# A selective-scan kernel: states and channels are laid out 4 x 32 on the partitions, and TensorE makes the scan's input

## The chip, the cores and the metric

The kernel runs on one core of one Trainium2 chip. A core has five engines, each with its own instruction queue worked off in order: PE (TensorE, matrix products; its weight loads are listed apart as PEld), DVE (VectorE), ACT (ScalarE), POOL (GpSimd) and SP (SyncE, which here only issues transfers). They meet by semaphores alone. Data lie in SBUF (128 partitions) and, for what PE writes, in PSUM (128 partitions, 8 banks of 512 fp32 columns). The metric is the device time of one execution in microseconds; of several runs the median counts.

## The reference, cut to what matters

The input is `x` of 64 channels x 256 time steps x 128 frequencies. A first layer runs two stages of bidirectional Mamba blocks, one along time and one along frequency; a second layer, a convolutional LSTM, follows and isn't touched here. For each direction of each stage:

```
u  = x * rsqrt(mean(x^2)) * norm_w
x, z = split(u @ in_proj)                      # 128 channels each
x  = silu(depthwise_conv4(x))
dt, B, C = split(x @ x_proj)                   # 4, 16, 16
dt = softplus(dt @ dt_proj + bias)             # 128 channels
for t:  h = exp(dt_t * A) * h + dt_t * B_t * x_t     # 128 channels x 16 states
        y_t = sum over the 16 states of h * C_t
y  = (y + x * Dp) * silu(z)
out = y @ out_proj
```

For each token the recurrence has 128 channels x 16 states = 2,048 values. All is fp32.

## The kernel before

**Tiling.** A stage (`Stage`) has 32,768 tokens in 64 chunks of 512 tokens (2 sequences of 256 in the time stage, 4 of 128 in the frequency stage). A chunk has two directions `d`, and each direction 8 slots of 128 partitions x 1,024 columns, so 16 slots `S` a chunk, 1,024 a stage, 2,048 in all. On the partitions lie 16 states x 8 channels; a slot's two column halves `j` are two groups of channels, 512 tokens each. A direction's eight slots are numbered by `k` (0 to 3) and `r` (0, 1).

**What a slot needs.** `inputs` (L546): PE spreads `dt*x` (tile `dtx`, 128 channels x 512 tokens) over the 16 states with the constant 0/1 matrix `sel`, two products of 64 rows x 512 columns, into the PSUM tile `bx` (two banks, three buffers). `times_b` (L580) multiplies `bx` by `B`, which was spread over the partitions by a transfer; 24 of 32 slots do this on DVE. The other 8 are "swapped" (L556): ACT copies `bx` into the SBUF tile `dA`, POOL multiplies there, and the decays go into `bx` instead. `decays` (L561): ACT computes exp(dt*A) from `rep`, the step sizes replicated over the states by a transfer (`spread_dt`, L456; 512 KB, one per slot, 7 buffers), into one of four `dA` tiles; the first column of every sequence is set to zero so that sequences don't mix. `recur` (L590): one DVE scan over 1,024 columns makes `h` (5 buffers). `outputs` (L608): POOL multiplies `h` by `C`. `add_up` (L613), every second slot: PE sums the states with the matrix `fold` into the PSUM tile `y`, four products of 512 columns, each on its own 32-column tile of the array. After eight slots DVE's `gate` (L634) multiplies `y` by `zs`, and `close_a`, `close_b`, `keep` (L641 to L675) make the stage's output.

**What a chunk needs before.** `HEAD` (L70) is a table of (slot, step): the steps that prepare the next chunk, placed among the slots of the current one (16 is the next chunk's first slot). `load`, `squares`, `means`, `rms`, `normalise` make the normalised input; `project_x`, `project_z` the projections; `silus` loads ACT's silu table and applies it to both directions' `xs` and `zs`. Softplus is made from abs, relu, exp and ln on ACT and three identity products on PE that add the parts up (`softplus_a`, `softplus_b`, `softplus_sum`, L392 to L424). `dt_away` writes `dt` to DRAM, from where `spread_dt` fetches it; `times_x` (POOL) makes `dtx`; `project_bc` makes B and C and writes them to DRAM, from where `spread_bc` fetches them replicated. All transfers are issued by SP, in the program's order.

**Order.** `run` (L686) writes the order out by hand; nothing reorders it. At slot S it issues: times_b(S+1), recur(S), at S mod 8 = 2 the gate, outputs(S-1), inputs(S+2), decays(S+2), the table's steps of slot S, skip, add_up, close_a or close_b with keep, then the steps of slot S+0.5. Each engine works off its share in this order, so an instruction that waits holds all that stand behind it on its engine. In the slot of `silus` the decays of two slots go ahead, in the next slot none.

Other PSUM tiles come from `mm` (one bank; one buffer). `first` (L471) prepares the first chunk of each stage.

Of the kernel before, what the change touches and what calls it, by code (L numbers as in the profile page):

```python
# [42 lines left out]
DL = P // NS  # L43
NK = 4
NG = 4 * NK
# [13 lines left out]
NREP = 7  # L59
RESPOND = 6  # L60
NH = 5
LAG = 2
SWAPPED = (2, 5, 9, 14, 18, 21, 25, 30)
EXP_AND_LN = "natural_log_exp_and_others"
SILU = "silu_and_others"
EDGES = (0, 1, LF - 2, LF - 1)
# [5 lines left out]
    (-8.5, "squares"),  # L72
    (-4.5, "means"),
    (-4.5, "rms"),
    (-3, "normalise"),
    (0, "project_x", 0),
    (1.5, "project_z", 0),
    (4, "project_z", 1),
    (5, "project_x", 1),
    (5, "silus"),  # L80
    (7.5, "project_bc", 0),
    (8, "softplus_a", 0),
    (8.5, "softplus_b", 0),
    (8.5, "spread_bc", 0, 0),
    (10.5, "softplus_sum", 0),
    (10.5, "dt_away", 0),
    (11.5, "times_x", 0),
    (12, "spread_bc", 0, 1),
    (12, "spread_dt", 0, 0),
    (12, "spread_dt", 0, 1),  # L90
    (12.5, "project_bc", 1),
    (12.5, "spread_dt", 0, 2),
    (13, "softplus_a", 1),
    (13, "softplus_b", 1),
    (13.5, "spread_dt", 0, 3),
    (14.5, "spread_dt", 0, 4),
    (15, "softplus_sum", 1),
    (15.5, "dt_away", 1),
    (16, "spread_dt", 0, 5),
    (16.5, "spread_dt", 0, 6),  # L100
    (16.5, "spread_dt", 0, 7),
    (17, "spread_dt", 1, 0),
    (17.5, "spread_bc", 1, 0),
    (19, "spread_dt", 1, 1),
    (20.5, "times_x", 1),
    (21, "spread_dt", 1, 2),
    (22, "spread_dt", 1, 3),
    (23, "spread_bc", 1, 1),
    (23, "spread_dt", 1, 4),
    (24, "spread_dt", 1, 5),  # L110
    (26.5, "spread_dt", 1, 6),
    (26.5, "spread_dt", 1, 7),
)

SECOND = tuple(
    (max(slot, 16), *step) for slot, *step in HEAD if step[0] == "spread_dt" and step[1:] > [0, 3]
) + (
    (14, "softplus_a", 1),  # L120
    (15, "softplus_b", 1),
    (15, "softplus_sum", 1),
    (15, "dt_away", 1),
    (16, "spread_bc", 1, 0),
    (16, "spread_bc", 1, 1),
    (17, "times_x", 1),
)


class Mamba:  # L130
# [3 lines left out]
    def __init__(self, ctx, tc, cols, room, d):  # L134
# [4 lines left out]
        self.mask = cp.tile([P, 2, NK, DL], F32, name="mask")  # L139
        self.sel = cp.tile([P, 2, NK, P], F32, name="sel")  # L140
        self.fold = cp.tile([P, NK, 32], F32, name="fold")
# [4 lines left out]
        self.A = cols[:, 12 : 12 + 4 * NG].rearrange("p (i g) -> p i g", i=4)  # L146
# [78 lines left out]
    def spreads(self):  # L225

        nc, mask = self.nc, self.mask
        nc.vector.tensor_add(mask.rearrange("p r k d -> p (r k d)"), self.ident[:, 0:C], self.ident[:, C:P])
        for r in range(2):
            for k in range(NK):  # L230
                nc.vector.tensor_copy(
                    self.sel[:, r, k].rearrange("p (s d) -> p s d", s=NS),
                    mask[:, r, k].unsqueeze(1).to_broadcast([P, NS, DL]),
                )

    def folds(self, ps):

        nc = self.nc
        pf = ps[:, 0 : 32 * NK].rearrange("p (k n) -> p k n", k=NK)
        for k in range(NK):  # L240
            nc.tensor.matmul(
                pf[:, k], lhsT=self.sel[0:32, 0, k], rhs=self.ident[0:32, 0:32], start=True, stop=True
            )
        nc.vector.tensor_copy(self.fold, pf)
# [13 lines left out]
class Stage:  # L258
# [8 lines left out]
    def __init__(self, ctx, m, stage, L, X, src, moments, gates):  # L267
# [12 lines left out]
        self.ps_mm = ctx.enter_context(tc.tile_pool(name=n + "mm", bufs=1, space=PSUM))  # L280
        self.ps_bx = ctx.enter_context(tc.tile_pool(name=n + "bx", bufs=3, space=PSUM))
        self.ps_y = ctx.enter_context(tc.tile_pool(name=n + "y", bufs=1, space=PSUM))

# [3 lines left out]
        self.zeros = fixed.tile([P, 2, self.nseq, 1], F32, name="zeros", tag="zeros")  # L287
        nc.gpsimd.memset(self.zeros, 0.0)
        self.dA = []
        for k in range(NRING):  # L290
            self.dA.append(fixed.tile([P, 2, self.nseq, L], F32, name=f"dA{k}", tag=f"dA{k}"))
# [76 lines left out]
    def project_x(self, ch, d):  # L368
        i = 2 * self.stage + d
        px = self.mm("px")  # L370
        xs = self.wk.tile([P, NTOK], F32, name="xs", tag="xs", bufs=3)
        self.shifted(px, i)
        self.nc.scalar.activation(xs, px, AF.Identity, bias=self.m.cb[:, i : i + 1])
        self.at["xs", ch, d] = xs

    def project_z(self, ch, d):
        pz = self.mm("pz")
        self.gated(pz, 2 * self.stage + d)
        zs = self.wk.tile([P, NTOK], F32, name="zs", tag="zs", bufs=4)
        self.nc.scalar.copy(zs, pz)  # L380
        self.at["zs", ch, d] = zs

    def silus(self, ch):
        nc = self.nc
        nc.scalar.preload_act_table_set(SILU)
        for n in ("xs", "zs"):
            for d in range(2):
                t = self.at[n, ch, d]
                nc.scalar.activation(t, t, AF.Silu)
        nc.scalar.preload_act_table_set(EXP_AND_LN)  # L390

    def softplus_a(self, ch, d):  # L392


        nc, m, wk = self.nc, self.m, self.wk
        i = 2 * self.stage + d
        pv = self.mm("pv")
        nc.tensor.matmul(pv, lhsT=m.Wdt[i], rhs=self.at["xs", ch, d], start=True, stop=True)  # L398
        e = wk.tile([P, NTOK], F32, name="e", tag="e")
        nc.scalar.activation(e, pv, AF.Abs, bias=m.dtb[:, i : i + 1])  # L400
        nc.scalar.activation(pv, pv, AF.Relu, bias=m.dtb[:, i : i + 1])
        nc.scalar.activation(e, e, AF.Exp, scale=-1.0)  # L402
        self.at["e", d], self.at["pv", d] = e, pv

    def softplus_b(self, ch, d):
        nc, wk = self.nc, self.wk
        w = wk.tile([P, NTOK], F32, name="w", tag="w")
        lw = wk.tile([P, NTOK], F32, name="lw", tag="lw")
        nc.scalar.activation(w, self.at["e", d], AF.Identity, bias=1.0)
        nc.scalar.activation(lw, w, AF.Ln)  # L410
        nc.scalar.activation(w, w, AF.Identity, scale=-1.0, bias=1.0)  # L411
        self.at["w", d], self.at["lw", d] = w, lw

    def softplus_sum(self, ch, d):

        nc, pv = self.nc, self.at["pv", d]
        parts = [self.at[n, d] for n in ("e", "w", "lw")]
        for n, t in enumerate(parts):
            nc.tensor.matmul(  # L419
                pv, lhsT=self.m.ident, rhs=t, start=False, stop=n == len(parts) - 1, skip_group_check=True  # L420
            )
        dt = self.wk.tile([P, NTOK], F32, name="dt", tag="dt", bufs=2)
        nc.scalar.copy(dt, pv)  # L423
        self.at["dt", d] = dt  # L424

    def dt_away(self, ch, d):

        there = self.dram.tile([32, 2, 2, NTOK], F32, name="there", tag="there")
        for r in range(4):
            self.nc.sync.dma_start(out=there[:, r % 2, r // 2], in_=self.at["dt", d][32 * r : 32 * r + 32])  # L430
        self.at["there", ch, d] = there

    def times_x(self, ch, d):
        dtx = self.wk.tile([P, NTOK], F32, name="dtx", tag="dtx", bufs=3)
        self.nc.gpsimd.tensor_mul(dtx, self.at["dt", d], self.at["xs", ch, d])  # L435
        self.at["dtx", ch, d] = dtx

    def project_bc(self, ch, d):
# [4 lines left out]
        self.nc.scalar.copy(t, pb)  # L443
        away = self.dram.tile([NBC, NTOK], F32, name="away", tag="away")
        self.nc.sync.dma_start(out=away, in_=t)
        self.at["away", ch, d] = away

    def spread_bc(self, ch, d, h):
        t = self.wk.tile([P, NTOK], F32, name="BC"[h], tag="BC"[h], bufs=3)
        away = self.at["away", ch, d]  # L450
        self.nc.sync.dma_start(
            out=t, in_=away[NS * h : NS * (h + 1)].unsqueeze(1).to_broadcast([NS, DL, NTOK])
        )
        self.at["BC"[h], ch, d] = t

    def spread_dt(self, ch, d, n):  # L456
        k, r = divmod(n, 2)
# [3 lines left out]
            out=t, in_=there[DL * k : DL * (k + 1), r].unsqueeze(0).to_broadcast([NS, DL, 2, NTOK])  # L461
        )
        self.at["rep", ch, d, n] = t
# [7 lines left out]
    def first(self):  # L471
# [4 lines left out]
        banks = [self.ps_bx.tile([P, 2, NTOK], F32, name="bx", tag="bx") for _ in range(3)]  # L476
# [10 lines left out]
        if time:  # L487
            m.dt(0, self.mm("pw"))
            m.load(False)
        x, z = {}, {}  # L490
        for d in range(2):
            x[d] = self.wk.tile([P, NTOK], F32, name="xs", tag="xs", bufs=3)
            z[d] = self.wk.tile([P, NTOK], F32, name="zs", tag="zs", bufs=4)
            self.at["xs", 0, d], self.at["zs", 0, d] = x[d], z[d]
        self.shifted(banks[0][:, 0], s)
        nc.scalar.activation(x[0], banks[0][:, 0], AF.Silu, bias=m.cb[:, s : s + 1])
        nc.scalar.preload_act_table_set(EXP_AND_LN)
        self.softplus_a(0, 0)
        if time:
            m.decay()  # L500
            m.spreads()
# [3 lines left out]
        self.softplus_b(0, 0)  # L505
        self.spare = [banks[0][:, 1]]
# [756 lines left out]
```

## Time and profile before

| | us |
|---|---|
| median of 3 runs | 7327.76 (7315.61 to 7332.9) |
| span of the profiled execution | 7324.0 |
| first scan's start to the last's | 48.7 to 6629.7 |
| ConvLSTM, after the second stage | from about 6640 to the end |
| PE busy | 6510.4 (89%) |
| DVE busy | 6924.8 (95%) |
| ACT busy | 6119.2 (84%) |
| POOL busy | 6703.3 (92%) |

The profile gives one execution. Its groups of instructions show the line, engine, operation, the tile written and those read, the shapes and the count; after the bar the busy time and the mean duration in ns; after the next bar the engine's idle time just before these instructions and what ended it. The timeline lists instructions in order of time: start, length (of several in a row together), engine, line, operation, tiles and count, and in brackets the idle time before it and what released it. An fp32 product shows as two MATMUL and two LDWEIGHTS instructions, here called its two halves. Matmuls overlap in the array, and a duration includes the filling of the pipe, so start-to-start distances tell what they cost. "64*128 64x512" is a product on a tile of 64 rows by 128 columns of the array, with 512 columns streamed.

### The profile page before, as it was taken

The numbers are of one execution on the slowest core, as the hardware profiler recorded it, in microseconds if no ns is written. First come the engines' busy times: TensorE is split into PE (matmuls) and PEld (weight loads), VectorE is DVE, ScalarE is ACT, GpSimd is POOL, SyncE is SP. The second block draws the span as 40 slices with busy tenths as digits, with TensorE's granted clock in tenths as the row PEclk, the third lists the DMA queues.
The fourth block names the chain that finished last, engine by engine and source line by source line (L and its number), as shares of the span: only waits on it lengthen the run. The fifth ranks groups of instructions, "written<-read, shape, count | busy, mean of one in ns | idle before, by whom it ended". The sixth has DMA issues, their size and how long they took to land. (4 is left out here: it accounts for less than half of the span.)

```text
span 7324.0 us, 86482 instructions
## 1 busy us (share of the span) xinstructions
PE 6510.4 (89%) x25104; PEld 2254.8 (31%) x25104; DVE 6924.8 (95%) x4684; ACT 6119.2 (84%) x11092; POOL 6703.3 (92%) x3410
## 2 busy tenths in 40 slices
PE   8888888888888888887898898888888888888999
PEld 2222222222222222222222222222222222226887
DVE  7999999999999999997999999999999999996887
ACT  7888889888898888987999999988998989983333
POOL 6999999999999999997999999999999999995554
PEclk9999999999999999999999999999999999999999
DMA  7888888888888888886888888878888788882000
GB/s 171 206 206 208 199 210 204 205 207 205 210 203 209 206 204 207 204 210 159 208 211 209 210 215 200 208 197 202 206 201 204 199 209 198 205 202 62 15 15 17
DMA packets 505887, 1359.47 MB, mean 186 GB/s; under 512 B 72772, under 2 KB 129732, under 8 KB 505416
## 3 DMA queue, kind: packets, MB, share of 16 engines
q1 hardware_dynamic: 505416, 1353.93, 74.6%
q8 instruction: 205, 3.36, 0.2%
q14 instruction: 266, 2.18, 0.1%
HBM read 1228.34 MB, written 92.27 MB: 180 GB/s over the span
## 5 line engine op out<-in xcount | busy, mean ns | idle before, releaser
L611 POOL TENSOR_TENSOR h<-h,C 128x1024 f32<-128x1024 f32 x2048 | 4797.5, 2366 | 32.4 <-DVE h L598 22.0
L598 DVE TENSOR_TENSOR_SCAN h<-dA,bx 128x1024 f32<-128x1024 f32 x1536 | 3443.8, 2269 | 0.0
L553 PE MATMUL bx<-dtx,sel 64*128 64x512 f32 x8192 | 2578.7, 653 | 364.8 <-DVE h L598 362.5
L588 DVE TENSOR_TENSOR bx<-bx,B 128x1024 f32<-128x1024 f32 x1536 | 1863.7, 1213 | 178.8 <-PE bx L553 178.2
L576 ACT ACTIVATE dA<-rep,cols 128x510 f32<-128x510 f32 (+1 forms) x3072 | 2021.7, 710 | 11.3 <-DMA rep<-there 11.3
L585 POOL TENSOR_TENSOR dA<-dA,B 128x1024 f32<-128x1024 f32 x512 | 1205.9, 2355 | 161.9 <-ACT dA L570 155.8
L553 PEld LDWEIGHTS bx<-dtx,sel 64*128 64x128 f32 x8192 | 733.3, 190 | 1888.1 <-issue 1070.5
L620 PE MATMUL y<-h,fold 128*32 128x512 f32 x8192 | 1239.5, 618 | 12.6 <-POOL h L611 10.9
L598 DVE TENSOR_TENSOR_SCAN h<-bx,dA 128x1024 f32<-128x1024 f32 x512 | 1167.9, 2281 | 15.4 <-POOL dA L585 15.4
L570 ACT COPY dA<-bx 128x1024 f32<-128x1024 f32 x512 | 518.5, 1013 | 352.7 <-PE bx L553 338.0
L576 ACT ACTIVATE bx<-rep,cols 128x510 f32<-128x510 f32 (+1 forms) x1024 | 705.5, 689 | 33.7 <-ACT bx L573 0.4
L398 PE MATMUL pv<-xs,wdt 128*128 128x512 f32 x512 | 341.2, 753 | 261.5 <-ACT bc L443 167.5
L620 PEld LDWEIGHTS y<-h,fold 128*32 128x32 f32 x8192 | 188.5, 109 | 933.5 <-issue 504.0
L435 POOL TENSOR_TENSOR dtx<-dt,xs 128x512 f32<-128x512 f32 x256 | 327.6, 1280 | 54.2 <-ACT dt L423 33.7
L364 PE MATMUL pz<-unp,wz 64*128 64x512 f32 x504 | 283.5, 642 | 91.0 <-ACT X L669 54.0
L360 PE MATMUL px<-unp,g 128*128 128x512 f32 x504 | 283.8, 644 | 9.5 <-DMA unp<-xn 7.0
L419 PE MATMUL pv<-e,ident 128*128 128x512 f32 x512 | 288.1, 645 | 3.4 <-ACT e L402 3.4
L441 PE MATMUL pb<-xs,wbc 128*32 128x512 f32 x504 | 260.9, 599 | 15.6 <-ACT made L809 15.6
L419 PE MATMUL pv<-w,ident 128*128 128x512 f32 x512 | 262.6, 594 | 6.1 <-ACT w L411 6.1
L419 PE MATMUL pv<-lw,ident 128*128 128x512 f32 x512 | 262.3, 594 | 0.0
L361 PE MATMUL px<-unp,g 128*128 128x512 f32 x504 | 257.8, 592 | 0.0
L1150 POOL TENSOR_TENSOR y<-v,X 128x512 f32<-128x512 f32 x32 | 40.6, 1270 | 230.7 <-DVE v L1148 230.7
(206 smaller groups left out, 7066.0 us busy)
## 6 DMA issues: line engine op xcount, KB each, us to landing
rep<-there SPq DMA_DIRECT2D x2048, 512.0 KB, 7.8
B<-away SPq DMA_DIRECT2D x256, 256.0 KB, 8.9
there<-dt SPq DMA_DIRECT2D x1024, 64.0 KB, 3.3
C<-away SPq DMA_DIRECT2D x256, 256.0 KB, 3.4
unp<-xn SPq DMA_DIRECT2D x504, 64.0 KB, 3.3
away<-bc SPq DMA_DIRECT2D x256, 64.0 KB, 4.1
u<-in_x SPq DMA_DIRECT2D x128, 64.0 KB, 8.9
out<-y SPq DMA_DIRECT2D x32, 256.0 KB, 2.0
```

The source lines that it names most:

```text
L360: nc.tensor.matmul(self.seqs(px), lhsT=m.G1[i], rhs=self.unp[:, :, first : first + L], start=True, stop=False)
L398: nc.tensor.matmul(pv, lhsT=m.Wdt[i], rhs=self.at["xs", ch, d], start=True, stop=True)
L419: nc.tensor.matmul(pv, lhsT=self.m.ident, rhs=t, start=False, stop=n == len(parts) - 1, skip_group_check=True)
L435: self.nc.gpsimd.tensor_mul(dtx, self.at["dt", d], self.at["xs", ch, d])
L553: self.nc.tensor.matmul(bx[:, j], lhsT=self.m.sel[rows, r, k], rhs=dtx[rows], start=True, stop=True)
L570: nc.scalar.copy(dA.rearrange("p j n l -> p j (n l)"), bx)
L576: nc.scalar.activation(dA[:, j, :, live], self.seqs(rep[:, j])[:, :, live], AF.Exp, scale=m.A[:, i, g : g + 1])
L585: self.nc.gpsimd.tensor_mul(bx, bx, b)
L588: self.nc.vector.tensor_mul(bx, bx, b)
L598: self.nc.vector.tensor_tensor_scan(h.rearrange("p j n -> p (j n)")[:, step], dA[:, step], bx[:, step], 0.0, ALU.mult, ALU.add,)
L611: self.nc.gpsimd.tensor_mul(h, h, self.at["C", ch, d].unsqueeze(1).to_broadcast([P, 2, NTOK]))
L620: nc.tensor.matmul(y[32 * r : 32 * r + 32], lhsT=m.fold[:, k], rhs=hs[r % 2][:, r // 2], start=False, stop=k == NK - 1, skip_group_check=True,
```

## The change

The layout becomes 4 states x 32 channels on the partitions. A direction's eight slots are numbered `q` (0, 1) and `b` (0 to 3): `b` is a block of 32 channels, and a slot holds states 4j + 2q + g for j = 0 to 3 (partitions) and g = 0, 1 (columns). Its 1,024 columns are i (half of the tokens, one PSUM bank each), g, and 256 tokens as 4 groups `u` of 64.

- `times_b` and `swapped` go. PE makes dt*x*B in one go: `turn` transposes `dtx` (tokens onto the partitions, `dtxT`, copied to SBUF by ACT) and B (tile `bt` in PSUM); `diagonal` (DVE, four calls per direction, each 128 x 1,024) multiplies B's turned columns with a mask of two stacked 64 x 64 identities, which gives 64 x 64 diagonal blocks `D`. `inputs` then multiplies `dtxT` (64 tokens x 32 channels, the weights) with the diagonal blocks (64 x 128, streamed): 32 products of 128 columns per slot on tiles of 64 rows by 32 columns, of which the array has eight.
- `bx` has two buffers instead of three, `mm` two instead of one, `bt` one: the eight banks are full.
- `spread_dt`: a replicated tile holds two channel blocks and serves four slots; two transfers per direction instead of eight (3 buffers). `spread_c` fetches C as 128 x 1,024, two per direction; B is not fetched. `dtx` and `bc` are written in the order (u, i, c); `away` is written by four transfers instead of one.
- `add_up` comes every fourth slot and adds four slots: 8 products of 512 columns on four column tiles, two on each. It is issued ahead of the table's steps. `h` has 7 buffers instead of 5.
- Softplus is ACT's own function with a table load of its own: one activation per direction; the identity products go. Both directions' `pv` products follow `silus` directly (`step_sizes`).
- `HEAD` is written anew; `silus` stands at slot 4 instead of 5.

```diff
-NREP = 7
+NREP = 3
-NH = 5
+NH = 7
...
 HEAD = (
...
+    (-2, "project_x", 0),
+    (-1, "project_z", 0),
+    (-1, "project_z", 1),
+    (0, "project_x", 1),
+    (4, "silus"),
+    (4, "step_sizes"),
+    (5, "softplus"),
+    (6, "project_bc", 0),
+    (6, "dt_away", 0),
+    (6.5, "dt_away", 1),
+    (7, "times_x", 0),
+    (8.5, "spread_dt", 0, 0),
+    (9, "spread_c", 0, 0),
+    (10, "turn", 0),
+    (11, "diagonal", 0, 0, 0),
+    (12, "spread_dt", 0, 1),
+    (12, "project_bc", 1),
+    (12.5, "times_x", 1),
+    (13, "diagonal", 0, 0, 1),
+    (13.5, "spread_c", 0, 1),
+    (15, "diagonal", 0, 1, 0),
+    (17, "diagonal", 0, 1, 1),
+    (17.5, "spread_dt", 1, 0),
+    (17.5, "spread_c", 1, 0),
+    (18, "turn", 1),
+    (19, "diagonal", 1, 0, 0),
+    (20, "spread_dt", 1, 1),
+    (21, "diagonal", 1, 0, 1),
+    (21.5, "spread_c", 1, 1),
+    (23, "diagonal", 1, 1, 0),
+    (25, "diagonal", 1, 1, 1),
...
-        self.ps_mm = ctx.enter_context(tc.tile_pool(name=n + "mm", bufs=1, space=PSUM))
-        self.ps_bx = ctx.enter_context(tc.tile_pool(name=n + "bx", bufs=3, space=PSUM))
+        self.ps_mm = ctx.enter_context(tc.tile_pool(name=n + "mm", bufs=2, space=PSUM))
+        self.ps_bx = ctx.enter_context(tc.tile_pool(name=n + "bx", bufs=2, space=PSUM))
...
+    def soft(self, ch, d):
...
+        self.nc.scalar.activation(dt, self.at["pv", d], AF.Softplus, bias=self.m.dtb[:, i : i + 1])
...
+    def turn(self, ch, d):
...
+        for u in range(NU):
+            own = slice(P * u, P * (u + 1))
+            nc.tensor.transpose(pt[:, own], dtx[:, own], m.ident)
+        for u in range(NU):
+            nc.tensor.transpose(bt[:, u], bc[0:NS, P * u : P * (u + 1)], m.ident[0:NS, 0:NS])
+        t = self.wk.tile([P, NU, P], F32, name="dtxT", tag="dtxT", bufs=2)
+        nc.scalar.copy(t.rearrange("p u d -> p (u d)"), pt)
...
+    def diagonal(self, ch, d, q, h):
...
+        self.nc.vector.tensor_mul(
+            D,
+            self.m.mask.unsqueeze(1).unsqueeze(1).to_broadcast([P, n, 2, W]),
+            b.unsqueeze(3).to_broadcast([P, n, 2, W]),
+        )
...
     def inputs(self, S):
...
-        for j in range(2):
-            rows = slice(C * j, C * j + C)
-            self.nc.tensor.matmul(bx[:, j], lhsT=self.m.sel[rows, r, k], rhs=dtx[rows], start=True, stop=True)
+        bx = self.ps_bx.tile([P, 2, 2, NU, W], F32, name="bx", tag="bx")
+        for u in range(NU):
+            for j in range(NJ):
+                for i in range(2):
+                    rows = slice(W * i, W * (i + 1))
+                    self.nc.tensor.matmul(
+                        bx[DB * j : DB * (j + 1), i, :, u],
+                        lhsT=dtxT[rows, u, DB * b : DB * (b + 1)],
+                        rhs=D[rows, u, j],
+                        start=True,
+                        stop=True,
+                    )
...
     def add_up(self, S):
...
+        for g in range(2):
+            for b in range(NB):
+                nc.tensor.matmul(
+                    y[DB * b : DB * (b + 1)].rearrange("p (i t) -> p i t", i=2),
+                    lhsT=self.m.fold,
+                    rhs=hs[b][:, g],
...
-            if 0 <= S + 1 < last:
-                self.times_b(S + 1)
...
+            if S % 4 == 1 and 4 < S <= last + LAG:
+                self.add_up(S - LAG)
```

## The prediction

> **What bounds the kernel now.** I read the page's first two parts, then the groups of instructions, then the waits of DVE, then the timeline of a few slots.
>
> ```profile
> span 7324.0 us, 86482 instructions
> ...
> PE 6510.4 (89%) x25104; PEld 2254.8 (31%) x25104; DVE 6924.8 (95%) x4684; ACT 6119.2 (84%) x11092; POOL 6703.3 (92%) x3410
> ...
> L611 POOL TENSOR_TENSOR h<-h,C 128x1024 f32<-128x1024 f32 x2048 | 4797.5, 2366 | 32.4 <-DVE h L598 22.0
> L598 DVE TENSOR_TENSOR_SCAN h<-dA,bx 128x1024 f32<-128x1024 f32 x1536 | 3443.8, 2269 | 0.0
> ...
> L588 DVE TENSOR_TENSOR bx<-bx,B 128x1024 f32<-128x1024 f32 x1536 | 1863.7, 1213 | 178.8 <-PE bx L553 178.2
> ...
> L585 POOL TENSOR_TENSOR dA<-dA,B 128x1024 f32<-128x1024 f32 x512 | 1205.9, 2355 | 161.9 <-ACT dA L570 155.8
> ```
>
> DVE and POOL are both nearly full; the multiplication by B, which the change takes away, sits on both (1,536 times on DVE, 512 on POOL). DVE's only large wait is for PE's `bx`, 178 us. The scans tell the length of a chunk (16 slots):
>
> ```profile
> L598 DVE TENSOR_TENSOR_SCAN h<-dA,bx x1536: 2256/2273/2285, 48.7 to 6629.7; 128x1024 f32<-128x1024 f32 x192
> ```
>
> From 48.7 to 6629.7 us is 6,581 us, or 51.4 us for each of 128 chunks. The timeline gives what one instruction really costs, from its start to the next one's:
>
> ```profile
> 3001.61 0.67 DVE L636 TENSOR_TENSOR yz<-y,zs 128x512 f32<-128x512 f32 x1
> ...
> 3002.19 1.22 DVE L588 TENSOR_TENSOR bx<-bx,B 128x1024 f32<-128x1024 f32 x1
> ...
> 3003.19 1.13 PE L553 MATMUL bx<-dtx,sel 64*128 64x512 f32 x4
> ...
> 3003.32 2.28 DVE L598 TENSOR_TENSOR_SCAN h<-dA,bx 128x1024 f32<-128x1024 f32 x1
> ...
> 3004.25 1.06 PE L620 MATMUL y<-h,fold 128*32 128x512 f32 x8
> ...
> 3005.24 0.70 PE L327 MATMUL pm<-sq,ones 128*128 128x256 f32 x2
> ...
> 3005.51 1.21 DVE L588 TENSOR_TENSOR bx<-bx,B 128x1024 f32<-128x1024 f32 x1
> ...
> 3006.63 4.45 DVE L598 TENSOR_TENSOR_SCAN h<-dA,bx 128x1024 f32<-128x1024 f32 x2
> ...
> 3006.93 1.04 PE L441 MATMUL pb<-xs,wbc 128*32 128x512 f32 x2
> ```
>
> A scan takes 2.19 (3003.32 to 3005.51), a B multiplication 1.12 (to 3006.63), a gate 0.58. A chunk has 16 scans, 12 B multiplications on DVE and 2 gates: 35.0 + 13.4 + 1.2 = 49.6 us. So 1.8 us of 51.4 is idle, about 0.3 of that the pause between the stages. POOL has 16 x 2.37 + 4 x 2.36 + 2 x 1.28 + 0.73 = 50.7 us: the two are balanced. How DVE comes to wait is seen here:
>
> ```profile
> 2077.19 2.07 PE L398 MATMUL pv<-xs,wdt 128*128 128x512 f32 x2 [1.82 <-ACT bc L443]
> ...
> 2079.19 1.73 PE L553 MATMUL bx<-dtx,sel 64*128 64x512 f32 x4
> ...
> 2080.97 1.23 DVE L588 TENSOR_TENSOR bx<-bx,B 128x1024 f32<-128x1024 f32 x1 [1.23 <-PE bx L553]
> ```
>
> PE runs in order: a `pv` product that waits for ACT holds the `bx` behind it, and DVE loses 1.23 us, even with three `bx` buffers.
>
> **The change, what DVE and POOL gain.** The 12 multiplications go; 8 `diagonal` calls come, each a 128x1024 tensor_tensor with one operand in PSUM like L588, so 1.12 each (from 1.08, twice the 0.54 by which it exceeds a gate of half the columns, to 1.22, L588's whole duration). DVE's chunk: 35.0 + 9.0 + 1.2 = 45.2 us, 4.4 less. POOL's falls to 37.9 + 2.6 + 0.7 = 41.2: no bound. If idle time stayed as it is, the kernel would save 128 x 4.4 = 563 us.
>
> **What ACT and the queues gain.** The swapped slots' four copies (1.04) go, and six of seven softplus instructions (about 0.6 each, twice), against one table load more (1.28) and two copies of `dtxT` (0.58). ACT was 84% busy: off the path by itself, but see below. Replicated step sizes fall from 16 transfers of 512 KB a chunk to 4; B's 2 go; C's 2 of 256 KB become 4 of 512 KB; `away` is written in 8 issues, not 2; SP issues some 30 where it issued some 36. ACT waited 11.3 us in all for `rep`, so this is worth that at most.
>
> **What PE pays.** A call of `inputs` was two products of 512 columns (four instructions: an fp32 product is two, each with a weight load). It becomes 32 products of 128 columns on 64x32 tiles, so 64 instructions and 64 loads. Two halves of one product take 0.86 of streaming (successive L419 products start at 3001.38 and 3002.24), 0.43 a half; L1027 at 240 columns is 160.5/768 = 0.21. Both scale to 0.107 for 128 columns. Each of eight tiles has 8 halves: 0.86 us if the eight run side by side, 6.9 us if none do. No row shows eight. The nearest: the fold's eight halves on four column tiles take 1.06 where the same shape on one tile (L441, two halves) takes 1.04; `bx`'s four on two row tiles take 1.13, as two of L360 do. Both directions overlap whole, so I take 0.87, and keep 1.72 (four at a time) and 6.9 as ends. An `inputs` call holds PE 1.06 now (3003.19 to 3004.25); it would hold it 1.06 - 0.86 + 0.87, about 1.1.
>
> The Trainium skill, "TensorE: Matmul & The Clock Gate", Part 3 (packing small matmuls), speaks against it: matmuls start and end in strict program order, only weight loads are pulled ahead. By that rule a product's second half would hold the tiles behind it, 32 x 0.11 = 3.5 us a call, an estimate that makes the kernel about 11.4 ms. The fold's row disagrees: in order it would need over 1.7 us, not 1.06. Part 1 (the clock gate) of the same page states a floor of about 25 ns between matmul starts: 64 x 0.025 = 1.6 us, an estimate that adds 5 x 0.73 us to the chain below and gives some 7,930 us.
>
> **The new wait.** `bx` has two buffers where it had three, so `inputs(S+2)` starts only when scan S ends; and there is work on PE and ACT that must follow in order. Per chunk the longest such row goes from the end of scan 0 to the start of scan 7. On PE: inputs 1.1, project_x 1.92 (2066.09 to 2068.01 in the timeline), inputs 1.1, add_up (two products on each of four tiles: 0.99 + 0.86 = 1.85), inputs 1.1, turn (eight halves of 128 columns 0.86 + 0.2, and four narrow ones; 1.4, between 0.6 and 1.9), close_a (0.86 + 2 x 0.43 + 0.2 = 1.92), inputs 1.1, close_b 1.0: 12.5 us. Then ACT: keep 0.95 (L661, two), the decays of slots 6 and 7 (four, 2.55), table load 1.29, first silu 0.62: 5.4. Then PE: two `pv` products 1.9, inputs(7) 1.1, add_up(3) 1.85, for scan 7 writes the `h` buffer (seven of them) that add_up(3) reads: 4.85. Four hand-overs of 0.12 (1.13 - 1.06 and 0.05 until the other engine starts) are 0.5, and the project_z ahead on PE costs some 0.5. Sum 23.8 us. DVE's own work in that stretch is 6 scans, 3 diagonals and a gate: 13.1 + 3.4 + 0.6 = 17.1. It waits 6.7 us. Elsewhere PE has slack: its chunk is 16 x 1.07 + 23.7 (fold 7.4, px 3.8, pz 2.1, pv 1.9, pb 2.1, means 0.6, turn 2.8, po 2.9, rounded) = 40.8 of DVE's 45.2.
>
> **The sum.** 45.2 + 6.7 + 0.3 (pause) + 0.3 (small waits, a third of today's) = 52.5 us a chunk, against 51.4: 128 x 1.1 = 141 us more. The span of 7,324.0 becomes 7,465; the median shown is 7,327.8, 3.8 above that span, so 7,469, which I give as 7,470. Prologue and the ConvLSTM (from 6,640 us on) keep their time within some 10 us.
>
> **Rivals.**
> Faster: the chain is shorter than I add up. It decides at 17.1 + 5.6 = 22.7 us, for then 45.2 + 5.6 + 0.6 is 51.4. With turn at 0.6 and neither hand-overs nor late start it is 22.0: 128 x 0.7 saves 90, 7,240. If add_up(3) is done in time, too, it is 20.2 and the stall 3.1: 48.9 us, 7,010; without any stall 6,610. For it: the chain is only 1.1 us above the point. Against it: 0.87 for `inputs` is already the floor.
> Eight tiles run four at a time: 1.72 + 0.2 a call; PE's chunk is 16 x 1.92 + 23.7 = 54.4, and it still waits some 4 us for ACT and DVE: 58.7, so 7,328 + 128 x 7.3 = 8,260. For it: nothing here shows loads and matmuls at 128 in 3 us (the ConvLSTM has 5,330 in 564 us, 9 a us). Against it: the fold's rows.
> No overlap between halves of different products: 3.5 a call, 23.7 + 16 x 3.7 = 83 us, 11.4 ms. Against it, again the 1.06.
> Hidden anyway: PE's extra work falls into DVE's scans and the chain just balances, within 0.2% (what a measurement of this kernel can tell from no change, 15 us, is 0.1 us a chunk).
>
> **How the numbers follow.** Forecast 0.52 (its own range 7,350 to 7,750: the chain from 22.9 to 26), faster 0.26, four at a time 0.14, no overlap 0.05, balance 0.03. Slower is 0.52 + 0.14 + 0.05 = 0.71. From 7,130 to 8,250 leaves out a third of the faster case and most of the two slow tile cases, 0.19 to 0.2.
>
> **What the profile will show.** The `inputs` line has 131,072 matmuls; if I am right about the tiles, 64 of them lie within about 1.1 us. The diagonals take 1.2 each, 1,024 of them. DVE's wait is put down to PE at the scan, once a chunk, at slot 7, for some 5 to 7 us; PE's wait to ACT's silu of `xs` at `pv`. POOL and the DMA share fall (DMA to half). I am wrong if `inputs` calls take 2 us or more, if PE's instructions come in late (gaps inside a call), or if slot 7 comes without a gap.

## The result, and the profile after

The changed kernel takes 7879.8 us (median; 7858.0 to 7885.2), the kernel before it 7324.9 in the same series: the ratio is 1.0748 (95% interval 1.0729 to 1.0767). The forecast was 7,470, slower by 141 us; it is slower by 555. The first lines of the page:

```profile
span 7880.5 us, 324564 instructions
...
PE 6410.5 (81%) x148488; PEld 3602.5 (46%) x148488; DVE 6363.7 (81%) x4166; ACT 4921.4 (62%) x8918; POOL 5571.1 (71%) x2898
...
PEclk8889999988899898988999898999889899998999
...
L583 DVE TENSOR_TENSOR_SCAN h<-dA,bx 128x1024 f32<-128x1024 f32 x2048 | 4614.8, 2275 | 1018.8 <-PE y L598 812.6
L555 PE MATMUL bx<-D,dtxT 64*32 64x128 f32 x131072 | 2578.3, 292 | 880.1 <-DVE h L583 872.5
...
L444 DVE TENSOR_TENSOR D<-mask,bt 128x1024 f32<-128x1024 f32 x1026 | 1226.0, 1195 | 9.7 <-PE bt L431 9.7
...
L363 PE MATMUL pv<-xs,wdt 128*128 128x512 f32 x512 | 452.2, 1035 | 510.3 <-ACT xs L357 508.8
```

DVE does less (6,364 us instead of 6,925) and stands still more; no engine is full. The waits of DVE (engine, line, what it waited for; us in all, times, longest) say for whom:

```profile
DVE h L583 <- PE y L598: 812.6, 166, 7.9
DVE yz L614 <- PE y L598: 291.2, 249, 4.4
DVE h L583 <- ACT dA L575: 198.4, 68, 13.0
```

Most of it is for `y`, the fold of `add_up`; the second line, the gate's wait, was not in the forecast at all. Where the waits lie in a chunk is read best from the distances between the starts of successive scans. This table is worked out from the trace: the mean, over the 56 middle chunks of each of the two stages, of the distance from scan n to scan n+1 of a chunk (column n). Columns that show DVE's own work to within 0.2 us are left out (e7 alone has more there, 4.0 us a chunk in all); the first row is that own work (scan 2.20, diagonal 1.11, gate 0.58), 45.2 us a chunk.

| kernel | us | chunk | 0 | 2 | 6 | 7 | 8 | 10 | 14 |
|---|---|---|---|---|---|---|---|---|---|
| DVE's own work | | 45.2 | 2.20 | 2.78 | 2.20 | 3.31 | 2.20 | 2.78 | 2.20 |
| changed kernel | 7880 | 55.5 | 2.36 | 3.82 | 9.11 | 3.32 | 2.20 | 4.17 | 3.05 |
| e1, PE kept at work | 7631 | 53.4 | 2.29 | 3.84 | 7.23 | 3.32 | 2.20 | 3.93 | 3.12 |
| e2, `pv` later | 7571 | 53.0 | 2.59 | 3.85 | 2.27 | 7.14 | 2.20 | 4.42 | 3.09 |
| e3, `add_up` ahead | 7758 | 54.6 | 2.24 | 3.05 | 9.88 | 3.32 | 2.20 | 2.78 | 3.66 |
| e5, eight `h` buffers | 7805 | 55.1 | 5.20 | 4.08 | 7.33 | 3.32 | 2.56 | 2.89 | 2.21 |
| e6, ACT ahead | 7796 | 54.8 | 2.25 | 4.08 | 7.57 | 3.32 | 2.20 | 4.39 | 3.55 |
| e7, `inputs` twice | 9785 | 70.4 | 3.81 | 6.46 | 10.29 | 3.32 | 2.37 | 6.74 | 5.93 |
| e8, four moves | 7571 | 53.1 | 6.08 | 4.67 | 2.29 | 3.30 | 3.60 | 2.78 | 2.67 |
| e9, transfers in four parts | 7842 | 55.3 | 2.34 | 3.82 | 9.06 | 3.32 | 2.20 | 4.17 | 2.91 |
| e10, e8 and e9 together | 6896 | 47.8 | 2.20 | 3.33 | 2.28 | 3.30 | 3.62 | 2.78 | 2.69 |
| e11, e5 and e9 together | 7484 | 52.5 | 2.80 | 3.92 | 7.42 | 3.32 | 2.54 | 2.81 | 2.20 |
| e12, e2, e3 and e9 together | 7324 | 51.2 | 2.25 | 3.17 | 2.20 | 7.56 | 2.20 | 3.25 | 3.04 |
| e13, e10 with `pb` later | 6901 | 47.8 | 2.20 | 3.32 | 2.28 | 3.30 | 3.58 | 2.78 | 2.75 |

The changed kernel's excess of 10.3 us a chunk lies in column 6 (6.9: ahead of scan 7), 2 (1.0: first gate), 10 (1.4: second gate), 14 (0.85: scan 15) and 0 (0.2). Two stretches of its timeline show how (start, length, engine, line, operation, tiles and count; in brackets the idle time before it and what released it). First the wait ahead of scan 7:

```profile
2288.88 1.15 PE L555 MATMUL bx<-D,dtxT 64*32 64x128 f32 x64 [0.48 <-DVE h L583]
...
2293.98 3.78 PE L363 MATMUL pv<-xs,wdt 128*128 128x512 f32 x4 [3.96 <-ACT xs L357]
...
2297.69 1.96 PE L555 MATMUL bx<-D,dtxT 64*32 64x128 f32 x64
...
2299.58 1.92 PE L598 MATMUL y<-h,fold 128*32 128x512 f32 x16
...
2301.62 2.29 DVE L583 TENSOR_TENSOR_SCAN h<-dA,bx 128x1024 f32<-128x1024 f32 x1 [7.40 <-ACT dA L575]
```

PE stands still for 4 us until ACT's silu, then `pv`, `inputs(7)` and `add_up(3)` follow in order, and scan 7 starts 0.12 us after the last. (The wait is named after ACT because the decays of slot 8 end at the same moment; those of slot 7 were done at 2292.0.) `inputs` took 1.15 us at 2288.88 and 1.96 after the standstill, `pv` 3.78 where the forecast had 1.9. The windows of that stretch tell why (each line has a stretch and its length; for PE, PEld, DVE, ACT and POOL the busy time, and in brackets the instructions; then the granted clock, the DMA share and GB/s):

```profile
2294.00:2296.00 2.00, 2.00 (x3) 0.96 (x4) 0.22 (x1) 1.98 (x4) 1.70 (x1) 0.50 0.26 102
2296.00:2298.00 2.00, 2.00 (x19) 0.49 (x25) 0.00 (x0) 1.63 (x3) 1.08 (x2) 0.50 0.25 102
...
2300.00:2302.00 2.00, 2.00 (x56) 0.82 (x56) 0.38 (x1) 1.58 (x4) 0.00 (x0) 1.00 0.08 33
```

Second, the gate at slot 10:

```profile
2251.63 1.20 DVE L444 TENSOR_TENSOR D<-mask,bt 128x1024 f32<-128x1024 f32 x1
2251.77 1.96 PE L555 MATMUL bx<-D,dtxT 64*32 64x128 f32 x64 [1.02 <-DVE h L583]
2252.75 2.28 DVE L583 TENSOR_TENSOR_SCAN h<-dA,bx 128x1024 f32<-128x1024 f32 x1
2253.66 2.63 PE L598 MATMUL y<-h,fold 128*32 128x512 f32 x16
...
2256.40 0.69 DVE L614 TENSOR_TENSOR yz<-y,zs 128x512 f32<-128x512 f32 x1 [1.38 <-PE y L598]
```

`inputs(11)` may start only when scan 9 ends, since `bx` has two buffers; `add_up(7)` stands behind it. DVE has a diagonal and scan 10 to do meanwhile, 3.3 us. At full clock the two calls take 3.1 us and would just be covered; here they take 4.5, for the clock is at half again:

```profile
2248.33:2251.74 3.41, 1.16 (x64) 0.89 (x64) 3.41 (x3) 3.36 (x7) 2.48 (x2) 1.00 0.50 120
2251.74:2255.15 3.41, 3.38 (x72) 1.90 (x76) 3.29 (x2) 0.00 (x0) 2.62 (x3) 0.50 0.26 55
```

All 112 middle chunks agree. In 5 of them the clock was full from the end of scan 9 to the end of the fold, and the gate didn't wait at all; in the 107 others it waited 1.04 to 2.38 us, 1.34 on average. Scan 15, which waits for `add_up(11)` to free its `h` buffer, was 0.01 us late on average in the 61 chunks in which the clock was full from the end of scan 12 on, and 1.69 us in the 51 others.

### The profile page after: what moved, and what is told of

Read it like the earlier page. It is cut to its first block, busy times and chain, and to the rows that moved or that the text cites. A ratio compares the mean times of both kernels' runs of the same rounds, so it can differ in the third digit from the quotient of the medians.

```text
span 7880.5 us, 324564 instructions
## 1 busy us (share of the span) xinstructions
PE 6410.5 (81%) x148488; PEld 3602.5 (46%) x148488; DVE 6363.7 (81%) x4166; ACT 4921.4 (62%) x8918; POOL 5571.1 (71%) x2898
## 3 DMA queue, kind: packets, MB, share of 16 engines
q1 hardware_dynamic: 300616, 674.33, 25.3%
## 4 chain that ended last, share of the span: by engine, by line
PE 33%; DVE 9%; ACT 5%; issue 4%; DMA 1%; POOL 1%; SPq 0%; DVEq 0%; POOLq 0%; ACTq 0%
PE bx L555 9%; DVE h L583 7%; PE cv L1003 6%; PE y L598 5%; PE pv L363 3%; ACT dA L575 2%; DVE D L444 2%; PE px L328 2%; PE pz L332 2%; PE px L329 1%; ACT L353 1%; ACT X L647 1%; PE po L629 1%; PE po L623 1%; POOL h L589 1%
## 5 line engine op out<-in xcount | busy, mean ns | idle before, releaser
L583 DVE TENSOR_TENSOR_SCAN h<-dA,bx 128x1024 f32<-128x1024 f32 x2048 | 4614.8, 2275 | 1018.8 <-PE y L598 812.6
L555 PE MATMUL bx<-D,dtxT 64*32 64x128 f32 x131072 | 2578.3, 292 | 880.1 <-DVE h L583 872.5
L555 PEld LDWEIGHTS bx<-D,dtxT 64*32 64x32 f32 x131072 | 1994.9, 112 | 2351.7 <-DVE h L583 1007.3
L575 ACT ACTIVATE dA<-rep,cols 128x510 f32<-128x510 f32 (+1 forms) x4096 | 2657.0, 709 | 12.0 <-DVE h L583 6.0
L444 DVE TENSOR_TENSOR D<-mask,bt 128x1024 f32<-128x1024 f32 x1026 | 1226.0, 1195 | 9.7 <-PE bt L431 9.7
L598 PE MATMUL y<-h,fold 128*32 128x512 f32 x8192 | 1085.1, 648 | 6.0 <-POOL h L589 6.0
L363 PE MATMUL pv<-xs,wdt 128*128 128x512 f32 x512 | 452.2, 1035 | 510.3 <-ACT xs L357 508.8
L341 ACT ACTIVATE xs<-px,cols 128x512 f32<-128x512 f32 x252 | 173.6, 689 | 573.7 <-PE px L329 573.7
L614 DVE TENSOR_TENSOR yz<-y,zs 128x512 f32<-128x512 f32 x256 | 176.9, 691 | 291.2 <-PE y L598 291.2
L572 ACT COPY dA<-zeros 128x4 f32<-128x4 f32 (+1 forms) x1024 | 194.9, 190 | 3.3 <-DVE h L583 3.2
L373 ACT ACTIVATE dt<-pv,cols 128x512 f32<-128x512 f32 x256 | 172.5, 687 | 25.3 <-issue 20.5
```

The source lines that it names most:

```text
L363: self.nc.tensor.matmul(pv, lhsT=self.m.Wdt[i], rhs=self.at["xs", ch, d], start=True, stop=True)
L444: self.nc.vector.tensor_mul(D, self.m.mask.unsqueeze(1).unsqueeze(1).to_broadcast([P, n, 2, W]), b.unsqueeze(3).to_broadcast([P, n, 2, W]),)
L555: self.nc.tensor.matmul(bx[DB * j : DB * (j + 1), i, :, u], lhsT=dtxT[rows, u, DB * b : DB * (b + 1)], rhs=D[rows, u, j], start=True, stop ...
L575: nc.scalar.activation(dA[:, :, g, :, live], rep[:, :, :, live], AF.Exp, scale=m.A[:, k, n : n + 1])
L583: self.nc.vector.tensor_tensor_scan(h[:, step], dA[:, step], bx[:, step], 0.0, ALU.mult, ALU.add)
L598: nc.tensor.matmul(y[DB * b : DB * (b + 1)].rearrange("p (i t) -> p i t", i=2), lhsT=self.m.fold, rhs=hs[b][:, g], start=False, stop=q == ...
```

## The experiments

Theories: the chain theory of the forecast (DVE waits where a row of ordered work on PE, and on ACT ahead of it, is longer than its own); as rivals, that PE has too much to do wherever it stands, so that waits only move, and that the clock alone is to blame. Column numbers are those of the table; what the expectations call the wait at slot 7 is column 6, and the one of scan 15 is column 14.

**e1: PE kept at work while it waits for ACT**

```diff
-    def step_size(self, ch, d):
+    def step_size(self, ch, d, extra=0):
...
         self.at["pv", d] = pv = self.mm("pv")
+        for _ in range(extra):
+            self.nc.tensor.matmul(
+                pv, lhsT=self.m.ident, rhs=self.unp.rearrange("p n l -> p (n l)")[:, 0:NTOK], start=True, stop=True
+            )
...
-            self.step_size(ch, d)
+            self.step_size(ch, d, 0 if d else 4)
```

> Four more 128x128 products of 512 columns stand ahead of the first pv product and write into the same PSUM tile, which pv then overwrites; they need nothing of ACT, so PE has 3.4 us of work in the 4.0 us in which it stood still there. Clock theory (the standstill is followed by a stretch at half the granted clock, in which two pv products took 3.78 instead of 1.9 us and inputs 1.96 instead of 1.16): pv 1.9, inputs 1.16, slot 7 comes 2.6 us sooner, 128 x 2.6 = 330 us less, about 7,550. Rival (the clock falls for another reason, such as the load over a longer time, or pv is slow in itself): nothing gained, 7,880 to 7,930, the longer end if the extra products hold up pv by 0.4 us.

7631.2 us, ratio 1.0421 (1.0401 to 1.0440): 249 us sooner, with 1,008 more matmul instructions. The same place in its windows, and its group of `pv` products:

```profile
1663.70:1665.70 2.00, 1.93 (x6) 0.69 (x6) 0.31 (x1) 1.98 (x5) 1.61 (x1) 1.00 0.25 102
1665.70:1667.70 2.00, 2.00 (x77) 1.20 (x80) 0.00 (x0) 1.99 (x3) 1.09 (x2) 1.00 0.26 106
```

```profile
L367 PE MATMUL pv<-xs,wdt 128*128 128x512 f32 x512 | 255.2, 620 | 59.0 <-ACT xs L357 57.5 <-ACT xs L500 1.6
```

The clock is full, a `pv` instruction has a mean of 620 ns instead of 1,035, and column 6 falls by 1.9. So the half clock at `pv` comes of the standstill; 1.9 of the 2.6 us expected came. Column 10 fell by only 0.24: in 103 of the 112 chunks the clock was still at half there.

**e2: `pv` behind `inputs(7)`**

```diff
-    (4, "step_sizes"),
+    (5, "step_sizes"),
```

> The pv products are issued one slot later, behind inputs(7) and add_up(3). Chain theory (scan 7 is late only because inputs(7) and add_up(3) stand behind pv, which waits for ACT's silu): scan 7 follows scan 6 at once; the next late one is scan 8, for ACT's decays(8) come behind softplus and its table load, at about 2301.5 in the profiled chunk where scan 8 began at 2304.9: 3.4 us a chunk, 440 us less, about 7,440. Rival 1 (PE has too much to do in a chunk wherever it stands): the waits only move, 7,850 or more. Rival 2 (ACT's row is as long as PE's): under 1 us a chunk, 7,750 or more, and the wait is at slot 8, put down to ACT.

7571.2 us, 1.0329 (1.0310 to 1.0348): 309 us sooner, 440 expected. Scan 7 follows at once (column 6: 2.27), and scan 8 is late in its place, by 3.8 us:

```profile
1658.59 1.33 ACT L575 ACTIVATE dA<-rep,cols 128x510 f32<-128x510 f32 x2
...
1660.00 4.46 DVE L583 TENSOR_TENSOR_SCAN h<-dA,bx 128x1024 f32<-128x1024 f32 x2 [3.69 <-POOL h L589]
```

The decays of slot 8 end at 1659.9 and the scan starts at 1660.0; the POOL instruction that the profile names ends then too, but works on `h` of slot 7, which scan 8 doesn't touch. So PE's row was the longest and ACT's the next, 3 us behind it.

**e3: `add_up` ahead of `inputs`**

```diff
+            if S % 4 == 1 and 4 < S <= last + LAG:
+                self.add_up(S - LAG)
             if 0 <= S + 2 < last:
                 self.inputs(S + 2)
...
-            if S % 4 == 1 and 4 < S <= last + LAG:
-                self.add_up(S - LAG)
```

> add_up is issued ahead of inputs in its slot, not behind. Theory of the small waits (inputs(S+2) starts at the end of scan S and takes 1.16, add_up then 1.9, together more than the scan of 2.2 that covers them; so the gates at slots 2 and 10 and the scan at slot 15, which needs an h buffer, wait about 1 us each): the waits of 1.4 and 1.15 us at slots 10 and 14 go, the one of 1.1 at slot 2 goes but comes back at slot 7, since it lies in the same row of PE: 2.5 us a chunk, 320 us less, about 7,560. Rival (PE's amount of work): waits only move, 7,850.

7758.1 us, 1.0595 (1.0577 to 1.0613): 122 us sooner, 320 expected. The gates wait no more (columns 2 and 10: 1.39 gone at 10), and what left column 2 came back in 6, as expected. But column 14 grew to 3.66: there `inputs(15)` now stands behind `add_up(11)`, and in all 112 chunks the clock was at half for part of that stretch. For the first gate (column 2), which stands at full clock in both kernels, the cause is shown: the order. For the second it isn't shown by this run: the expectation reckons with a cover of 2.2 us, but the trace has 3.3, and together with the order the clock changed, for between scans 8 and 11 it is at half for 1% of the time instead of 47%. e5 parts the two.

**e5: eight `h` buffers**

An eighth buffer alone has no room in SBUF (e4: a pool needs 18.125 KB a partition where 16.78 are left), so two other tiles give up theirs.

```diff
-NH = 7
+NH = 8
...
-        xn = self.io.tile([P, n, L], F32, name="xn", tag="xn")
+        xn = self.rs
...
-        dev = self.io.tile(list(x.shape), F32, name="dev", tag="dev")
+        dev = self.io.tile(list(x.shape), F32, name="dev", tag="sq")
```

> h gets eight buffers instead of seven (xn is written over rs, and dev shares the buffer of sq, to make room in SBUF). Chain theory: scan 7 no longer waits for add_up(3), 1.9 us behind inputs(7), and scan 15 not for add_up(11), 1.1 us: 3.0 us a chunk, 384 us less, about 7,500; the gates' waits stay. Rival (PE's amount of work): the wait moves to the next slots, 7,820 or more. Since the run with add_up ahead kept only 0.95 of the 2.5 us a chunk that were expected, a value between, about 7,600, would mean that half of such a gain is lost again to PE's next stand at half clock.

7804.7 us, 1.0658 (1.0623 to 1.0693): 75 us sooner, 384 expected. The waits on `add_up` go where they should (columns 6 and 14 by 1.8 and 0.85; scan 15 isn't late even in the 50 chunks with the clock at half ahead of it). Column 10 falls by 1.3, too, though the second gate's order is as it was and its wait was expected to stay: here the clock was full at that gate in 104 of the 112 chunks, and it waited in none of them; in the 8 others it waited 1.42. So the wait of column 10 comes of the half clock. That makes 3.9 us in all (the table's row is of the profiled execution, 7,834 us, the longest of four), and a wait of 2.8 stands in column 0, where there was hardly one. Taken alone that speaks for "waits only move"; e9 to e11 find what it is.

**e6: ACT three slots ahead**

```diff
-NRING = 4
+NRING = 5
...
-            for ahead in ((2, 3) if S % 16 == silu else () if S % 16 == silu + 1 else (2,)):
-                if 0 <= S + ahead < last:
-                    self.decays(S + ahead)
+            if 0 <= S + 3 < last:
+                self.decays(S + 3)
```

with the room as in e5.

> ACT works three slots ahead instead of two (five dA tiles, decays(S+3) in every slot; room as in the run with eight h buffers). Theory of ACT's row (pv is late because ACT's silu comes behind keep and four decays in its queue): two decays fewer stand ahead of silu, so pv and with it scan 7 come 1.3 us sooner, 170 us less, about 7,710. Rival (ACT is off the path, and pv waits for keep through PE's own row): 7,860 to 7,880.

7796.1 us, 1.0649 (1.0631 to 1.0667): 84 us sooner, 170 expected. Column 6 falls by 1.5, the 1.3 expected and a little more; columns 2, 10 and 14 take 1.0 of it back.

**e7: every `inputs` call twice**

```diff
-        for u in range(NU):
+        for u in [*range(NU), *range(NU)]:
```

> Every inputs call issues its 32 products twice (the second time over the same values), so a call holds PE 2.1 us instead of 1.16. Chain theory (PE counts where its row is longer than DVE's, and elsewhere a scan covers it): five calls lie in the row from scan 0 to scan 7, 5 x 0.97 = 4.9 us, one ahead of the gate of slot 10 and one ahead of scan 15, 1.9: 6.8 us a chunk, 870 us more, about 8,750; less, down to 8,550, if PE's fuller time keeps its clock up. Rival (PE's amount of work is the bound everywhere): 16 x 0.97 = 15.5 us a chunk, 9,860.

9785.2 us, 1.3366 (1.3343 to 1.3389): 14.9 us a chunk more, close to the rival's 15.5 and far from 6.8. The waits of PE hold a line that the changed kernel has for only 7 us:

```profile
PE bx L555 <- issue: 880.0, 903, 2.8
```

PE stood still 880 us, inside `inputs` calls, for nothing that the view of waits shows; 6.9 us a chunk, mostly at slots 9 to 15. The trace's transfers point at the supply of instructions (586,708 instead of 324,564): of the 903 stops, 896 ended 1.1 to 1.6 us after a packet of the queue that brings instructions had landed, where 12% of moments taken at random lie so. No run changes that supply alone. With these stops the chain theory comes to 13.7; but that sum leaves out what the fuller clock (0.97 instead of 0.91) should give back, and the run doesn't decide between the two theories. What it does show is where a longer `inputs` isn't hidden: columns 0, 2, 10 and 14 grow by 1.5 to 2.9 each, the columns left out of the table by 4.0 in all, columns 7 and 8 by less than 0.2.

**e8: four moves together**

```diff
-NRING = 4
+NRING = 5
...
-    (4, "silus"),
-    (4, "step_sizes"),
+    (3, "silus"),
+    (5, "step_sizes"),
```

with `add_up` as in e3, `decays` as in e6 and the room as in e5.

> Four moves together: ACT three slots ahead (five dA tiles), silus one slot sooner (ahead of keep), pv one slot later (behind inputs(7)), add_up ahead of inputs; room as in the run with eight h buffers. Chain theory: the wait ahead of slot 7 (6.9 us) goes, the gates' waits go, and what is left is about 1 us at slot 2 to 3 and 1.5 at slot 14 plus up to 2 us at slot 8 or 9 for ACT: 49 to 50.5 us a chunk instead of 55.5, 7,050 to 7,250, sooner than the kernel before the change. Rival (PE's or ACT's amount of work is the bound): the waits come back elsewhere, 7,450 or more.

7571.0 us, 1.0342 (1.0327 to 1.0358): the waits of columns 6 and 10 are gone, and the rival's time came all the same, for column 0 has 3.9 us of wait and column 2 has 1.9. The waits of PE say what is late:

```profile
PE px L328 <- DMA unp<-rs: 451.1, 124, 9.7
```

The transfer into `unp`, which `px` reads, is issued three slots earlier and landed 8 us later in the chunk looked at. Ahead of it in the queue stood two replicated transfers of 512 KB. In the changed kernel's trace, 4,096-byte packets run four at a time for 66% of the time from 1000 to 3000 us, about 25 a us, so that 512 KB take 5.1 us; in the kernel before it is most often sixteen (27% of the time).

**e9: the replicated transfers in four parts, alone**

```diff
-        self.nc.sync.dma_start(out=t, in_=away.unsqueeze(1).to_broadcast([NJ, DB, 2 * NTOK]))
+        for j in range(NJ):
+            self.nc.sync.dma_start(
+                out=t[DB * j : DB * (j + 1)], in_=away[j : j + 1].to_broadcast([DB, 2 * NTOK])
+            )
...
-        self.nc.sync.dma_start(
-            out=t, in_=there[:, 2 * h : 2 * h + 2].unsqueeze(0).to_broadcast([NJ, DB, 2, NTOK])
-        )
+        for j in range(NJ):
+            self.nc.sync.dma_start(out=t[DB * j : DB * (j + 1)], in_=there[:, 2 * h : 2 * h + 2])
```

> spread_dt and spread_c are issued as four transfers of 32 partitions each instead of one of 128. In the trace of the changed kernel the packets of one replicated transfer (128 of 4,096 bytes) run four at a time, about 25 a us (512 KB in 5.1 us), where those of the kernel before run sixteen at a time; a transfer whose first dimension is 32 instead of 4 should spread over all sixteen. Theory (in the changed kernel these transfers are hidden; its PE waits only 28 us in all for transfers): 7,840 to 7,890. Rival (their slowness already costs time): 7,780 or less.

7841.8 us, 1.0703 (1.0688 to 1.0719): 38 us sooner. The packets now run up to sixteen at a time and none is under way for 61% of the time. In the changed kernel itself the slow transfers were hidden but for half a per cent.

**e10: e8 and e9 together**

> The four moves together, and the replicated transfers in four parts. In the run of the four moves alone a new wait of 3.3 us (stage 1) to 4.3 (stage 2) stood at the first slot of a chunk: px waited for the transfer into unp, which landed 8 us after it was issued, behind the replicated ones. Theory (it is these transfers' slowness): that wait goes, and about 1 us of the one at slot 2 that follows from it: 3.5 to 5 us a chunk, 6,950 to 7,130, sooner than before the change. Rival (PE's amount of work takes the place of that wait): 7,450 or more.

6895.8 us, 0.9413 (0.9397 to 0.9429): sooner than both kernels, by 12.5% and 5.9%, and 54 us below the lower end expected. Its page, and the same line of PE's waits as in e8:

```profile
span 6893.5 us, 328783 instructions
...
PE 5959.6 (86%) x148488; PEld 3490.4 (51%) x148488; DVE 6359.7 (92%) x4166; ACT 5070.6 (74%) x9300; POOL 5563.9 (81%) x2898
```

```profile
PE px L328 <- DMA unp<-rs: 8.1, 2, 4.3
```

The wait in column 0 goes whole, and 1.3 us of column 2 with it. So it wasn't PE's amount of work that took the place of the waits in e5 and e8, but a transfer. DVE is 92% busy; 2.6 us of wait are left in a chunk.

**e11: e5 and e9 together**

> Eight h buffers, and the replicated transfers in four parts, in the order of the changed kernel. Eight buffers alone took away 1.85 us at slot 7, 1.25 at slot 10 and 1.15 at slot 14, but a wait of 2.8 us at slot 0 and 0.4 at slot 2 stood in their place. Theory (that wait is for the transfer into unp): it goes, 128 x 2.8 = 360 us less than with eight buffers alone, 7,430 to 7,480. Rival (PE's amount of work): 7,750 or more.

7483.9 us, 1.0214 (1.0198 to 1.0229), at the upper edge of what was expected: 321 us sooner than e5, by 2.4 us in column 0. Eight buffers are worth 358 us once that obstacle is gone (against e9), and 75 while it stands.

**e12: the two changes of order and the transfers, no further buffer**

> From the changed kernel: pv one slot later, add_up ahead of inputs, replicated transfers in four parts; no further buffer, and silus and keep where they were. Theory (two rows in turn: with PE's row freed, ACT's is next, keep, four decays, silu, softplus and two table loads ahead of decays(8)): the wait of 3.7 us at slot 8, which the run with pv alone moved later had, stays, the gates' waits go: 2.5 us a chunk less than that run, about 7,250 (7,150 to 7,350). Rival (ACT's lead isn't needed once PE's row and the transfers are free): 6,900 to 7,000.

7323.7 us, 0.9996 (0.9986 to 1.0005), in the range of the theory of two rows: scan 8 is 4.2 us late for ACT (column 7: 7.56). In all 112 chunks scan 8 starts some 0.1 us after its decays. What separates this kernel from e10 is ACT's lead (a fifth `dA` tile and the room for it, silus ahead of keep): 428 us.

**e13: e10 with `project_bc` of the first direction one slot later**

```diff
-    (6, "project_bc", 0),
...
+    (7, "project_bc", 0),
     (7, "times_x", 0),
```

> The run with the four moves and the transfers in four parts, with project_bc of the first direction one slot later, behind inputs(9). There, PE waits 177 us in all ahead of pb for ACT's softplus, which frees the PSUM tile, and inputs(8) behind it makes scan 9 late by 1.2 us a chunk. Theory: that wait goes, 128 x 1.2 = 155 us less, about 6,740. Rival (pb's own followers, B and C for the next chunk, come late instead, or the wait passes to the next product): 6,870 to 6,950.

6901.1 us, 0.9418 (0.9403 to 0.9432): nothing gained, column 8 stays at 3.6. In the chunk looked at, `pb` no longer held PE, and scan 9 started 0.1 us after its decays, which stand on ACT behind softplus and two table loads; it does so in all 112 chunks. In e10 it already did in 106 of them, with `inputs(9)` done 1.35 us ahead of the scan on average. So the premise was wrong: the wait was ACT's, not `pb`'s, and the move couldn't take it away.

## Why the prediction was right and wrong

- **What DVE gains: right.** 45.2 us a chunk were predicted and are its own work in the table; start-to-start a scan takes 2.20, a diagonal 1.11. The 563 us are there.
- **`inputs` at 1.1 us with all eight tiles side by side: right.** 64 instructions lie in 1.15 us at full clock; the rivals with four tiles at a time and with no overlap fall. The two estimates drawn from the Trainium skill, "TensorE: Matmul & The Clock Gate", Part 3 (strict order, as the forecast read it) and Part 1 (about 25 ns between starts), fall with them: first starts lie 6 to 7 ns apart (2288.880, 2288.887, 2288.893, 2288.900).
- **The chain to scan 7: mechanism right, size short.** 23.8 us were predicted; in the chunk shown it is 25.5 from the end of scan 0 (2276.1) to 2301.6, and on average columns 2 and 6 have 7.9 us of wait where 6.7 were predicted. The terms that failed are "two `pv` products 1.9" and "inputs(7) 1.1": they came at half clock, 3.78 and 1.96. Smaller terms went the other way (turn 0.9 instead of 1.4, the late start 0.3 instead of 0.5). `pv` and `inputs` were priced from rows at full clock; after the change `pv` comes behind a standstill of 4 us. e1 takes 1.9 us a chunk out of column 6. A row at half clock stood among the forecast's own lines: at 2077.19, behind a wait of 1.82, a single `pv` product took 2.07 us, and the `bx` behind it 1.73 instead of 1.13. The window of the kernel before has the clock, 0.50:

```profile
2077.19:2079.19 2.00, 2.00 (x2) 0.50 (x2) 2.00 (x2) 1.58 (x4) 2.00 (x2) 0.50 0.26 72
```

- **"0.3 (small waits, a third of today's)": wrong, and the larger part of the miss.** Columns 10, 14 and 0 have 2.4 us. The second gate and scan 15 each wait for an `add_up` that stands behind an `inputs`. At the forecast's prices the pair is hidden, but only just: 3.1 us under a diagonal and a scan, 3.3. What failed is again the clock that the price took for granted: at half clock the pair takes 4.5, and the wait is there in the chunks with the clock at half and next to nothing in the others (1.34 against none at the gate, 1.69 against 0.01 at scan 15; e5 has the clock full at the gate and no wait). "Elsewhere PE has slack", 40.8 of 45.2 us a chunk, was an average that hid places with next to nothing to spare. Column 0 (0.2 of the 2.4) stays unexplained.
- Together 1.2 + 2.1 = 3.3 us a chunk, 128 x 3.3 = 420 us; the miss is 555 - 141 = 414.
- **"This is worth that at most", of the transfers: right for this kernel** (e9: 38 us), where their share fell to a third (74.6% to 25.3%) for half the bytes. That the replicated ones have four packets under way instead of up to sixteen the forecast didn't see, and it cost 675 us as soon as the rest was put right (e8 to e10).
- **The faster rival** needed the chain at 22.7 us or less. Its mechanism (no wait for `add_up(3)`) is e5 and e11; alone it isn't enough.
- **What the profile would show:** the scan's wait for PE ahead of scan 7, PE's wait for silu (509 us) and no gaps inside calls came as said. The 249 waits of the gate did not stand there.

## What to carry to other kernels

Where a shared buffer lets a product start only at the end of a step, add up for every step what stands behind it in the same queue and compare it with the steps that cover it; an average of slack hides this. Do the sum at half clock, too, wherever PE waits ahead of it: here two places with at most 0.2 us to spare at full clock fell 1.3 us and more short at half. Fill the wait if the work behind it is urgent. When waits seem only to move, name the releaser of the new one before blaming the amount of work: here it was a transfer that had become slow unseen, and with it put right, four moves that had seemed to bring 3.9% (e8) brought 12.1% (e10 against e9).

## What the runs showed of the hardware that was not expected

- **The clock is decided on a grid.** All changes of the granted clock in the changed kernel's trace lie on a grid of 3.413 us, within 1 ns over the whole span. Of the grid's stretches at full clock between 100 and 7,150 us, 299 had PE busy for less than 45% of the time, and each was followed by half clock; of 71 with 45 to 50%, 9 were; of 1,301 with more, none. The kernel before has 46 of 46, 25 of 31 and none of 1,736; e10 has 53 of 53, 12 of 43, and 7 of 1,579 with more than 50%, so the edge isn't sharp. That makes 10.2 us at half clock in a middle chunk, against 2.4 in the kernel before and 2.2 in e10. The Trainium skill, "TensorE: Matmul & The Clock Gate", Part 1, names the same window of some 3.4 us and says that an idle one brings the half rate; these runs show that a window needn't be idle for it: in these three traces under 45% of work was always enough.
- **A leading dimension of four confines a transfer.** The replicated transfers, whose first dimension is 4, had four packets under way; the same bytes with a first dimension of 32 (e9) had up to sixteen, and none under way for 61% of the time instead of 18%. "DMA: Bandwidth & Descriptors", "Why a DMA increments its semaphore by 16 and not by 1", states this: the number of engines is the largest up to 16 that divides the slowest dimensions. The runs agree.
- **Many small products seem to outrun the supply of instructions.** On eight tiles the matmuls of an uninterrupted call start 14 ns apart on average at full clock (e7: 128 in 2.03 us; changed kernel: 64 in 1.15), close to the 0.107 / 8 = 13.4 ns of the forecast's sum. In e7, with calls of 128, PE stopped 903 times, 880 us in all, and 896 of the stops ended 1.1 to 1.6 us after a packet of instructions had landed; the changed kernel, with calls of 64, stopped there for 7 us in all.
